# Attention on uncentred features in a graph kernel: vT = xT + hT times column-centred weights, scaled per node at evacuation, and the s2 row as a product of ones with a diagonal

## The chip, the cores and the metric

The kernel runs on one core of a Trainium2 chip. The metric is the device time of one execution, in microseconds; a profile is one more execution of the same program.

## The reference, cut to what matters

There are 64 graphs of 256 nodes with 256 features. Each passes three gated graph layers (GRU), a residual with layer norm, then graph attention, again with residual and layer norm.

```python
# layer 0: three times: m = h @ weight[i]; aggr = A.T @ m; h = GRU(aggr, h)
x = _layernorm(x + h, axis=-1)                 # called y below
# layer 1
Wh = jnp.matmul(x, W)
s1 = jnp.einsum('bnf,f->bn', Wh, a[:Fout, 0])
s2 = jnp.einsum('bnf,f->bn', Wh, a[Fout:, 0])
e = jax.nn.leaky_relu(s1[:, :, None] + s2[:, None, :], negative_slope=0.2)
attn = jax.nn.softmax(jnp.where(adj > 0, e, -9e15), axis=2)
x = _layernorm(x + jnp.matmul(attn, Wh), axis=-1)
```

## The kernel before

Graphs go through in pairs: 32 pairs, each of 512 nodes. A pair is a generator that yields between steps; two pairs are under way, half a pair apart, so that TensorE works on one pair's gates while other engines finish a step of the other pair. The scheduler that compiles the kernel may still reorder instructions; where I speak of the compiled order, I mean its result.

```python
    # pools for PSUM: four banks "t" for transposes, aggregation, attention; four "g" for gates
    def gates(i, e, ag, hT, hT_new, name):      # one half (128 features) of a layer's gates
        hn = product(2 * C + e, [hid])          # 2 + 4 + 2 + 4 = 12 f32 matmuls of 512 columns
        r_p = product(e, [hid, inp])
        n_p = product(2 * C + e, [inp])
        z_p = product(C + e, [hid, inp])
        # ACT: r, n, z; DVE: n, d*z, hT_new; POOL: d = hT - n
    ...
    def pair(p):
        hT = to_T(x_sb, f"xT_{p}")              # eight TensorE transposes
        yield
        for i in range(L):
            ag = aggregate(h, A, ...)           # eight f32 matmuls of 256 columns
            for e in range(C):
                gates(i, e, ag, hT, hT_new, ...)
                yield
            ...                                 # from_T(hT): eight transposes back to [node, feature]
            # last layer: v = h + x at evacuation on DVE, y = layer_norm(v)
            yield
        yT = to_T(y, f"yT_{p}")                 # eight transposes
        yield
        s2 = bank("s2")
        for d in range(C):                      # wa2: W @ a2 broadcast over 128 columns
            nc.tensor.matmul(s2, wa2[:, d, :], yT[:, d, :], start=(d == 0), stop=(d == C - 1))
        for k in range(K):                      # K = 4 blocks of 128 nodes
            pt = bank("pwh")
            for d in range(C):
                nc.tensor.matmul(pt[:, :D + 1], yT[:, d, k * P:(k + 1) * P], gw[:, d, :], ...)
            ...                                 # s1 and wh evacuated; scores = s2 + s1 on ACT
        ...                                     # leaky relu, mask, max on DVE, exp on ACT
        yield
        ...                                     # eT: eight transposes
        yield
        ...                                     # po = eT.T @ wh; residual; layer norm; store

    steps = 3 + 3 * L + 2                       # 14
    active, started = [], 0
    while started < NP or active:               # the next pair starts when the one has done 7 steps
        if started < NP and (not active or (len(active) == 1 and active[0][1] >= steps // 2)):
            active.append([pair(started), 0])
            started += 1
        for a in list(active):                  # one step of each
            ...
```

## Time and profile before

The median was 2843.95 us in three runs. What matters of the profile:

| per pair, TensorE | matmuls in the code | spacing |
|---|---|---|
| gates | 72, f32, 512 columns | 0.86 us each |
| aggregation | 24, f32, 256 columns | 0.43 us each |
| wh (with s1) | 8, f32, 257 columns | 0.43 us each |
| output product | 8, f32, 256 columns | 0.43 us each |
| s2 | 2, f32, 512 columns | 0.86 us each |
| transposes | 48 of 128 columns, 8 of them for y | 0.109 us each |

Spacing is the time from the start of one matmul's record to the next one's. An f32 matmul of the code is two records. The profile's mean durations are longer (592 ns for a record of 512 columns), because records overlap; for a TensorE that is the bound it is the spacing that adds up to the time. The spacings of all records sum, by construction, to the time from the first matmul to the last. A group's median spacing is its work, and what lies above it is waiting.

### The profile page before, as it was taken

To read this page: it belongs to the slowest core of one execution; us is meant where nothing else is said; L and a number is where in the kernel's file an instruction comes from. 1 tells how busy PE (TensorE), PEld (TensorE's weight loads), DVE (VectorE), ACT (ScalarE), POOL (GpSimd) and SP (SyncE) were. 2 spreads that over 40 slices of the span, in tenths; PEclk is the share of its full clock that TensorE was granted. 3 is DMA by queue.
4 is the path that set the end of the run, shared out by engine and by line. 5 is a ranking of instruction groups with operands and counts; after the bars stand their busy time and mean duration, and the time that the engine had idled before them with its cause. 6 is when DMAs were issued, how large, how long until landed. Compare 5 with 4: busy or idle time off the path is not lost.

```text
span 2842.6 us, 23364 instructions
## 1 busy us (share of the span) xinstructions
PE 2803.1 (99%) x8928; PEld 1560.3 (55%) x8928; DVE 1185.5 (42%) x2387; ACT 776.6 (27%) x1357; POOL 358.0 (13%) x362
## 2 busy tenths in 40 slices
PE   7999999999999999999999999999999999999996
PEld 4555555555555555555555555555555555555554
DVE  2344444444443444434443444443444444434434
ACT  1223222222322223222323222222222222222231
POOL 1111111111111111111111111111111111111111
PEclk9999999999999999999999999999999999999998
DMA  3000000000000000000000000000000000000000
GB/s 89 8 15 23 15 23 15 15 23 22 15 16 22 15 22 15 23 15 17 21 23 15 23 15 15 23 19 19 15 23 15 23 15 23 15 15 15 8 0 15
DMA packets 53518, 54.44 MB, mean 19 GB/s; under 512 B 1696, under 2 KB 53408, under 8 KB 53408
## 3 DMA queue, kind: packets, MB, share of 16 engines
q1 hardware_dynamic: 52256, 51.91, 5.6%
q8 instruction: 70, 1.15, 0.2%
q10 hardware_dynamic: 1056, 1.05, 0.1%
q14 instruction: 40, 0.33, 0.0%
q0 software_dynamic: 96, 0.01, 0.0%
HBM read 36.18 MB, written 16.78 MB: 19 GB/s over the span
## 4 chain that ended last, share of the span: by engine, by line
PE 98%; DVE 1%; DMA 0%; ACT 0%; issue 0%; POOL 0%; SPq 0%; POOLq 0%; DVEq 0%; ACTq 0%
PE pg L191 69%; PE pa L181 12%; PE pwh L270 4%; PE po L303 4%; PE pt L171 3%; PE s L263 2%; PE pt L162 2%; PE pt L294 1%; PE pw L138 1%; DMA adj<-in_adj_dram 0%; DVE d L210 0%; ACT z L207 0%; DVE hT L211 0%; PE pw L126 0%; DVE v L307 0%
## 5 line engine op out<-in xcount | busy, mean ns | idle before, releaser
L191 PE MATMUL pg<-ag,wc 128*128 128x512 f32 x2304 | 1051.4, 592 | 0.0
L191 PEld LDWEIGHTS pg<-ag,wc 128*128 128x128 f32 x2304 | 437.8, 190 | 551.0 <-issue 551.0
L191 PE MATMUL pg<-hT,whhT 128*128 128x512 f32 x1536 | 712.0, 592 | 0.0
L191 PEld LDWEIGHTS pg<-hT,whhT 128*128 128x128 f32 x1536 | 281.9, 190 | 278.8 <-issue 275.0
L202 DVE SCALAR_TENSOR_TENSOR n<-pg,bh,r 128x512 f32<-128x512 f32 x192 | 143.9, 750 | 603.8 <-ACT r L199 603.8
L199 ACT ACTIVATE r<-pg,b_sum 128x512 f32<-128x512 f32 x192 | 131.9, 687 | 859.8 <-PE pg L191 859.4
L191 PE MATMUL pg<-xT,whhT 128*128 128x512 f32 x768 | 350.5, 592 | 0.0
L210 DVE TENSOR_TENSOR d<-d,z 128x512 f32<-128x512 f32 x192 | 132.6, 691 | 522.0 <-ACT z L207 450.0
L209 POOL TENSOR_TENSOR d<-hT,n 128x512 f32<-128x512 f32 x128 | 162.1, 1267 | 1041.4 <-ACT n L204 1041.4
L181 PE MATMUL pa<-A,h 128*128 128x256 f32 x1024 | 239.3, 382 | 0.0
L204 ACT ACTIVATE n<-n,bi 128x512 f32<-128x512 f32 x192 | 138.5, 722 | 349.2 <-DVE n L203 349.2
L191 PEld LDWEIGHTS pg<-xT,whhT 128*128 128x128 f32 x768 | 143.5, 190 | 155.2 <-issue 146.1
L207 ACT ACTIVATE z<-pg,b_sum 128x512 f32<-128x512 f32 x192 | 132.1, 688 | 322.0 <-PE pg L191 322.0
L181 PEld LDWEIGHTS pa<-A,h 128*128 128x128 f32 x1024 | 191.9, 190 | 51.1 <-DVE h L72 12.1
L209 POOL TENSOR_TENSOR d<-xT,n 128x512 f32<-128x512 f32 x64 | 81.0, 1266 | 563.0 <-ACT n L204 563.0
L203 DVE TENSOR_TENSOR n<-n,pg 128x512 f32<-128x512 f32 x192 | 132.2, 689 | 32.5 <-PE pg L191 26.0
L211 DVE TENSOR_TENSOR hT<-d,n 128x512 f32<-128x512 f32 x192 | 131.9, 687 | 3.4
L171 PEld LDWEIGHTS pt<-ident,hT 128*128 128x128 f32 x768 | 88.4, 141 | 52.6 <-DVE hT L211 31.6
L270 PE MATMUL pwh<-gw,yT 128*128 128x257 f32 x512 | 116.7, 380 | 0.0
L303 PE MATMUL po<-wh,eT 128*128 128x256 f32 x512 | 116.5, 381 | 0.0
L181 PE MATMUL pa<-A,x 128*128 128x256 f32 x512 | 115.7, 379 | 0.0
L270 PEld LDWEIGHTS pwh<-gw,yT 128*128 128x128 f32 x512 | 97.5, 190 | 28.3 <-issue 8.5
(84 smaller groups left out, 1860.4 us busy)
## 6 DMA issues: line engine op xcount, KB each, us to landing
x<-in_x_dram SPq DMA_DIRECT2D x32, 512.0 KB, 3.8
adj<-in_adj_dram SPq DMA_DIRECT2D x32, 512.0 KB, 3.9
out_dram<-o SPq DMA_DIRECT2D x32, 512.0 KB, 2.9
wi_n<-in_L_gnn_w_ih_dram SPq DMA_DIRECT2D x1, 768.0 KB, 6.6
w_n<-in_L_gnn_weight_dram ACTq DMA_DIRECT2D x1, 768.0 KB, 9.4
wh_n<-in_L_gnn_w_hh_dram SPq DMA_DIRECT2D x1, 768.0 KB, 11.1
gw<-in_L_gnn_W_dram ACTq DMA_DIRECT2D x1, 256.0 KB, 10.4
bi<-in_L_gnn_b_ih_dram POOLq DMA_DIRECT2D x1, 3.0 KB, 8.1
```

The source lines that it names most:

```text
L171: nc.tensor.transpose(pt[:, (c * C + d) * P:(c * C + d + 1) * P], hT[:, d, (g * C + c) * P:(g * C + c + 1) * P], ident)
L181: nc.tensor.matmul(pt[:, g * N:(g + 1) * N], h[:, g, s, d * P:(d + 1) * P], A[:, g, s, :], start=(s == 0), stop=(s == C - 1))
L191: nc.tensor.matmul(pt, w[:, d, o * P:(o + 1) * P], m[:, d, :], start=(n == 0), stop=(n == len(todo) - 1))
L199: nc.scalar.activation(r, r_p, AF.Sigmoid, bias=b_sum[:, e:e + 1])
L202: nc.vector.scalar_tensor_tensor(n, hn, bh[:, 2 * C + e:2 * C + e + 1], r, op0=ALU.add, op1=ALU.mult)
L203: nc.vector.tensor_add(n, n, n_p)
L204: nc.scalar.activation(n, n, AF.Tanh, bias=bi[:, 2 * C + e:2 * C + e + 1])
L207: nc.scalar.activation(z, z_p, AF.Sigmoid, bias=b_sum[:, C + e:C + e + 1])
L209: nc.gpsimd.tensor_sub(d, hT[:, e, :], n)
L210: nc.vector.tensor_mul(d, d, z)
L270: nc.tensor.matmul(pt[:, :D + 1], yT[:, d, k * P:(k + 1) * P], gw[:, d, :], start=(d == 0), stop=(d == C - 1))
L303: nc.tensor.matmul(pt[:, c * D:(c + 1) * D], eT[:, g, j, c * P:(c + 1) * P], wh[:, g, j, :], start=(j == 0), stop=(j == C - 1))
```

## The change

The intent is to take work off TensorE. Layer norm is (v - mean) / std per node, so y @ W is v @ (W with its column means removed), times 1/std per node. So wh can be had from vT = xT + hT, which is there without transposing y, and the per-node scale is applied when ACT evacuates the product. s2 has then to be scaled per node too; it comes as one more column of wh and is turned into a row, the same on all partitions, as ones @ diag(s2), in two float32r products (the value rounded to float32r, and what remains).

The core of the diff (comments, the weights' preparation and names are cut):

```diff
-    gw = const.tile([P, C, D + 1], F32, name="gw")
-    wa2 = const.tile([P, C, P], F32, name="wa2")
+    gw = const.tile([P, C, D + 2], F32, name="gw")
+    gwc = const.tile([P, C, D + 2], F32, name="gwc")       # gw less its column means
+    ones = const.tile([P, P], F32R, name="ones")
 ...
-            else:
-                from_T(hT, ...)                            # v = h + x
-                y = work.tile(...)
-                layer_norm(v, y, f"a_{p}")
             yield
-        yT = to_T(y, f"yT_{p}")
-        yield
-        s2 = bank("s2")
-        for d in range(C):
-            nc.tensor.matmul(s2, wa2[:, d, :], yT[:, d, :], ...)
+        vT = work.tile([P, C, GN], F32, tag="hT", name=f"vT_{p}", bufs=4)
+        for d in range(C):
+            nc.gpsimd.tensor_add(vT[:, d, :], hT[:, d, :], xT[:, d, :])
+        from_T(vT, lambda g, pt: evacuate(v[:, g]...., pt))
+        rs = layer_norm(v, y, f"a_{p}")
+        yield
         for k in range(K):
             pt = bank("pwh")
             for d in range(C):
-                nc.tensor.matmul(pt[:, :D + 1], yT[...], gw[:, d, :], ...)
-            nc.vector.tensor_copy(s1[:, k:k + 1], pt[:, D:D + 1])
-            evacuate(wh[:, k // C, k % C, :], pt[:, :D])
-            nc.scalar.activation(sc[:, k, :], s2[...], AF.Identity, bias=s1[:, k:k + 1])
+                nc.tensor.matmul(pt[:, :D + 2], vT[...], gwc[:, d, :], ...)
+            nc.scalar.activation(wh[:, k, :], pt[:, :D + 2], AF.Identity, scale=rs[:, k:k + 1])
+        yield
+        s2 = work.tile([P, 2, K], F32R, ...)
+        nc.gpsimd.tensor_copy(s2[:, 0], wh[:, :, D + 1])
+        nc.gpsimd.tensor_sub(s2[:, 1], wh[:, :, D + 1], s2[:, 0])
+        dg = work.tile([P, 2, K, P], F32R, tag="dg", bufs=1)
+        for half in range(2):
+            nc.gpsimd.tensor_mul(dg[:, half], <ident, broadcast>, <s2[:, half], broadcast>)
+        s2b = bank("s2b")
+        for half in (1, 0):
+            nc.tensor.matmul(s2b, ones, dg[:, half]...., start=(half == 1), stop=(half == 0))
+        for k in range(K):
+            nc.scalar.activation(sc[:, k, :], s2b[...], AF.Identity, bias=wh[:, k, D:D + 1])
```

xT gets buffers of its own, and em has one buffer instead of two. A pair now has 15 steps, while `steps` still says 14: the offset between two pairs is 7 and 8 in turn.

More of the change, by code (lines that the diff above doesn't have):

```diff
@@ L9 @@
 F32 = mybir.dt.float32
+F32R = mybir.dt.float32r
 U8 = mybir.dt.uint8
@@ L91 @@
     wc = const.tile([P, L, C, O], F32, name="wc")
-    gw = const.tile([P, C, D + 1], F32, name="gw")
-    wa2 = const.tile([P, C, P], F32, name="wa2")
+    gw = const.tile([P, C, D + 2], F32, name="gw")
+    gwc = const.tile([P, C, D + 2], F32, name="gwc")
+    ones = const.tile([P, P], F32R, name="ones")
+    mean = const.tile([P, P], F32, name="mean")
+    nc.gpsimd.memset(mean, 1.0)
+    nc.gpsimd.tensor_copy(ones, mean)
+    nc.gpsimd.memset(mean, 1.0 / D)
     b_sum = const.tile([P, O // P], F32, name="b_sum")
@@ L147 @@
                                  start=(f == 0), stop=(f == C - 1))
-            wa = prep.tile([P, 2], F32, name=f"wa_{d}")
-            nc.vector.tensor_copy(wa, pt[:, :2])
-            nc.vector.tensor_copy(gw[:, d, D:D + 1], wa[:, 0:1])
-            nc.vector.tensor_copy(wa2[:, d, :], wa[:, 1:2].to_broadcast([P, P]))
+            nc.vector.tensor_copy(gw[:, d, D:], pt[:, :2])
+        pt = bank("pw")
+        for d in range(C):
+            nc.tensor.matmul(pt[:, :D + 2], mean, gw[:, d, :], start=(d == 0), stop=(d == C - 1))
+        for d in range(C):
+            nc.vector.tensor_sub(gwc[:, d, :], gw[:, d, :], pt[:, :D + 2])
     def to_T(src, name):
-        dst = work.tile([P, C, GN], F32, tag="hT", name=name, bufs=4)
+        dst = work.tile([P, C, GN], F32, tag="xT", name=name, bufs=2)
         for d in range(C):
@@ L226, in layer_norm @@
                                     mv[:, k, 0:1], rs[:, k:k + 1], op0=ALU.subtract, op1=ALU.mult)
+        return rs
     def pair(p):
@@ L236, in pair @@
             load(p + 1)
-        hT = to_T(x_sb, f"xT_{p}")
+        hT = xT = to_T(x_sb, f"xT_{p}")
         yield
@@ L250, in pair @@
                 from_T(hT, lambda g, pt: evacuate(h[:, g].rearrange("p c d -> p (c d)"), pt))
-            else:
-                from_T(hT, lambda g, pt: nc.vector.tensor_add(
-                    v[:, g].rearrange("p c d -> p (c d)"), pt, x_sb[:, g].rearrange("p c d -> p (c d)")))
-                y = work.tile([P, G, C, D], F32, tag="y", name=f"y_{p}")
-                layer_norm(v, y, f"a_{p}")
-            yield
-        yT = to_T(y, f"yT_{p}")
-        yield
-        s2 = bank("s2")
-        for d in range(C):
-            nc.tensor.matmul(s2, wa2[:, d, :], yT[:, d, :], start=(d == 0), stop=(d == C - 1))
-        wh = work.tile([P, G, C, D], F32, tag="wh", name=f"wh_{p}")
-        s1 = work.tile([P, K], F32, tag="s1", name=f"s1_{p}")
-        sc = work.tile([P, K, N], F32, tag="sc", name=f"sc_{p}")
+            yield
+        vT = work.tile([P, C, GN], F32, tag="hT", name=f"vT_{p}", bufs=4)
+        for d in range(C):
+            nc.gpsimd.tensor_add(vT[:, d, :], hT[:, d, :], xT[:, d, :])
+        from_T(vT, lambda g, pt: evacuate(v[:, g].rearrange("p c d -> p (c d)"), pt))
+        y = work.tile([P, G, C, D], F32, tag="y", name=f"y_{p}")
+        rs = layer_norm(v, y, f"a_{p}")
+        yield
+        wh = work.tile([P, K, D + 2], F32, tag="wh", name=f"wh_{p}")
         for k in range(K):
@@ L269, in pair @@
             for d in range(C):
-                nc.tensor.matmul(pt[:, :D + 1], yT[:, d, k * P:(k + 1) * P], gw[:, d, :],
+                nc.tensor.matmul(pt[:, :D + 2], vT[:, d, k * P:(k + 1) * P], gwc[:, d, :],
                                  start=(d == 0), stop=(d == C - 1))
-            nc.vector.tensor_copy(s1[:, k:k + 1], pt[:, D:D + 1])
-            evacuate(wh[:, k // C, k % C, :], pt[:, :D])
-            nc.scalar.activation(sc[:, k, :], s2[:, (k // C) * N:(k // C + 1) * N], AF.Identity,
-                                 bias=s1[:, k:k + 1])
+            nc.scalar.activation(wh[:, k, :], pt[:, :D + 2], AF.Identity, scale=rs[:, k:k + 1])
+        yield
+        s2 = work.tile([P, 2, K], F32R, tag="s2", name=f"s2_{p}")
+        nc.gpsimd.tensor_copy(s2[:, 0], wh[:, :, D + 1])
+        nc.gpsimd.tensor_sub(s2[:, 1], wh[:, :, D + 1], s2[:, 0])
+        dg = work.tile([P, 2, K, P], F32R, tag="dg", name=f"dg_{p}", bufs=1)
+        for half in range(2):
+            nc.gpsimd.tensor_mul(dg[:, half], ident.unsqueeze(1).to_broadcast([P, K, P]),
+                                 s2[:, half].unsqueeze(2).to_broadcast([P, K, P]))
+        s2b = bank("s2b")
+        for half in (1, 0):
+            nc.tensor.matmul(s2b, ones, dg[:, half].rearrange("p k j -> p (k j)"),
+                             start=(half == 1), stop=(half == 0))
+        sc = work.tile([P, K, N], F32, tag="sc", name=f"sc_{p}")
+        for k in range(K):
+            nc.scalar.activation(sc[:, k, :], s2b[:, (k // C) * N:(k // C + 1) * N], AF.Identity,
+                                 bias=wh[:, k, D:D + 1])
         nc.vector.scalar_tensor_tensor(sc, sc, ALPHA, sc, op0=ALU.mult, op1=ALU.max)
-        em = work.tile([P, K, N], F32, tag="em", name=f"em_{p}")
+        em = work.tile([P, K, N], F32, tag="em", name=f"em_{p}", bufs=1)
         nc.gpsimd.memset(em, NEG_INF)
@@ L302, in pair @@
                 for j in range(C):
-                    nc.tensor.matmul(pt[:, c * D:(c + 1) * D], eT[:, g, j, c * P:(c + 1) * P], wh[:, g, j, :],
+                    nc.tensor.matmul(pt[:, c * D:(c + 1) * D], eT[:, g, j, c * P:(c + 1) * P], wh[:, g * C + j, :D],
                                      start=(j == 0), stop=(j == C - 1))
```

## The prediction

> **What bounds the kernel now.** I read the page first, its line of busy time and its chain that ended last:
>
> ```profile
> PE 2803.1 (99%) x8928; PEld 1560.3 (55%) x8928; DVE 1185.5 (42%) x2387; ACT 776.6 (27%) x1357; POOL 358.0 (13%) x362
> ...
> PE 98%; DVE 1%; DMA 0%; ACT 0%; issue 0%; POOL 0%; SPq 0%; POOLq 0%; DVEq 0%; ACTq 0%
> ```
>
> TensorE is the bound: it is 98% of the chain, and the other engines have more than half their time free. A busy PE need not be one at its peak, so I then looked at the spacing of matmuls in the timeline, PE only, in the middle of the span (columns: start us, us, engine, line, operation, names, count):
>
> ```profile
> 1526.80 1.88 PE L191 MATMUL pg<-xT,whhT 128*128 128x512 f32 x4
> 1528.51 1.88 PE L191 MATMUL pg<-ag,wc 128*128 128x512 f32 x4
> 1530.23 1.04 PE L162 MATMUL pt<-ident,y 128*128 128x128 f32 x8
> 1531.10 0.38 PE L171 MATMUL pt<-ident,hT 128*128 128x128 f32 x2
> 1531.32 1.02 PE L191 MATMUL pg<-hT,whhT 128*128 128x512 f32 x2
> 1532.18 1.02 PE L263 MATMUL s<-yT,wa 128*128 128x512 f32 x2
> 1533.23 0.87 PE L171 MATMUL pt<-ident,hT 128*128 128x128 f32 x6
> 1533.94 1.02 PE L263 MATMUL s<-yT,wa 128*128 128x512 f32 x2
> 1534.80 3.64 PE L270 MATMUL pwh<-gw,yT 128*128 128x257 f32 x16
> 1538.27 1.89 PE L181 MATMUL pa<-A,h 128*128 128x256 f32 x8
> ```
>
> Each f32 matmul is two records, 0.43 us apart for 512 columns, so 0.86 us for one in the code; the eight transposes take 0.87 us; nothing is idle between rows but 0.1-0.2 us. In PE's waits the only long ones are in the first 20 us and after the last pair's gates (4.6 us for y, 6.6 us for the exponentials). So 31 of 32 pairs run with their attention hidden behind the other pair's gates, and PE time removed is gained one for one, if PE doesn't come to wait.
>
> **What the Trainium skill says.** "FP8 and Floating Point Precision", TensorE Precision Notes: true FP32 takes four passes through the array, and there is a reduced-precision one. "TensorE: Matmul & The Clock Gate", Back-to-back issue gap: 512 columns take 512/2.4 + 2.5 = 216 ns a pass when warm. Four passes are 0.86 us: the trace agrees. No page prices float32r; I estimate one pass, 0.22 us. "GPSIMD Engine Reference", Elementwise side-by-side: a two-input tensor_tensor costs about 2.6 cycles an element, and some 156 ns to start: 512 x 2.6 / 1.2 GHz + 156 = 1265 ns by estimate; the trace has 1267 ns, so I use that for the new 128x512 operations. The first page also says that matmuls keep program order (the queue pulls only weight loads ahead); so a matmul that waits holds all behind it.
>
> **The change, part by part** (per pair unless said; 32 pairs). The shapes and counts of what goes (columns: line, engine, operation, names, shapes, count, busy us, mean ns, idle before):
>
> ```profile
> L209 POOL TENSOR_TENSOR d<-hT,n 128x512 f32<-128x512 f32 x128 | 162.1, 1267 | 1041.4 <-ACT n L204 1041.4
> ...
> L263 PE MATMUL s<-yT,wa 128*128 128x512 f32 x128 | 67.2, 609 | 0.5 <-ACT yT L70 0.5
> ...
> L162 PE MATMUL pt<-ident,y 128*128 128x128 f32 x256 | 34.1, 277 | 4.6 <-DVE y L225 4.6
> ```
>
> - Gone from PE: y's transposes, 0.87 us, and two f32 matmuls for s2, 2 x 0.86 = 1.72 us. Sum 2.59 us.
> - New on PE: two float32r matmuls of 512 columns, 2 x 0.22 = 0.44 us. The eight transposes of the last h become eight of vT; pwh's 257 columns become 258: nothing.
> - Net 2.15 us a pair, 69 us in all. Had PE no new wait, 2844 - 69 = 2775 us, 2.4% less.
> - Elsewhere: POOL gains two adds, two products (1.27 us each) and two small operations (0.23 us as its smallest have); DVE loses copies; all of wh's evacuation goes to ACT. Not one of these is near a bound.
> - Prologue: two matmuls for the column means and a subtraction, +1.5 us. Tail: the last pair's chain loses y -> yT -> s2 and gains vT's add and the diagonal; by the tail's rows I get about 2 us less. They cancel.
>
> **Where the gain leaks.** What counts is the new order of waits. The changed pair has 15 steps against 14, and the next starts when one has done at least 7, so the offsets of pairs alternate between 7 and 8. The compiled order shows two patterns in turn, 16 pairs with offset 7, 15 with offset 8, and the last alone. I walk each with the trace's durations; t = 0 is where the second gate product z of the partner's layer 0 has been issued (1530.23 above).
>
> Offset 8. PE: eight pwh matmuls to t = 3.47, eight transposes of h to 4.34, one gate matmul to 5.20, then the float32r product, all others behind it. It needs: last pwh out of PE, 3.67; ACT's evacuation, 0.48 (a 128x256 one with a bias takes 478 ns), 4.15; POOL copy and subtraction, 0.23 each with 0.08 between, 4.77; two 128x512 products, the first one not waiting for the subtraction's end, 1.27 each, 7.33; 0.1 to PE: 7.4. **PE waits 2.2 us.** The products run from the low half first on PE, so both must be there. Before, s2 came straight from yT and had no such loop. 15 x 2.2 = 33 us.
>
> Offset 7. The float32r product comes only after the partner's next 12 gate matmuls, over 10 us later: no wait. But the layer norm is now in the way: vT's transposes 0 to 0.87, v's copies on DVE to 2.34, the partner's last h to 3.03, then statistics and power, 3.1 us in the tail's rows (2807.11 to 2810.22): the per-node scale is there at 6.1, the first evacuation at 6.65. PE has finished pwh at 6.26 and its next product, the aggregation, needs that bank (four banks in turn): 0.4 us. The transposes of h wait 0.2 us as before the change they did not; the exponentials come later (9.8 us after s2b, with 10.3 us of gates to hide them), which delays z by about 1.3 us and makes the output product wait 0.2 us at most. Together 0.9 us. 16 x 0.9 = 14 us.
>
> Sum: 2844 - 69 + 33 + 14 = 2822 us.
>
> **The rivals.** (1) PE stays without waits: 2775 us. For it: the reorder puts other matmuls ahead of most new waits, and before the change nothing waited. Against: the offset-8 order has only 1.7 us of PE work between pwh and the float32r product, and the chain there is 3.9 us. If POOL's products took half the time, 2800. (2) The float32r product costs as much as an f32 one (four passes): +1.3 us a pair, of which nothing is hidden: 2860 or so; no record of the kernel before can exclude it. (3) POOL holds up the gates: it is in order, and now a memset of the single em buffer (it must wait for the exponentials) stands ahead of a gate's subtraction. At offset 7 my walk has the partner's h at 34.05 and PE asking for it at 34.2: no slack. A microsecond too many in it costs 16 us: 2840. (4) Load on DVE or ACT: at 42% and 27% of time, and DVE loses work; I see nothing for it.
>
> **Range and chances.** I name 2820. The low end, 2785, is half of the waits gone and a bit more; the high end, 2848, has a further 1 us a pair. To be faster by over 2% the time must be under 2787, so the waits would have to be 12 us in all rather than 47: 0.13. Slower by over 2% means above 2901, waits of 126 us, 4 us a pair, or a float32r at full cost with these: 0.02. Within 2%: 0.85.
>
> **What would show it.** y's transposes and the s2 group gone; float32r records 64, about 0.22 us apart; PE busy about 70 us less; among PE's waits one of about 2.2 us, 15 times, s2b for POOL's diagonal; one of about 0.4 us, 16 times, for ACT's evacuation of wh; POOL's products at 1.27 us. Wrong if the s2b waits are absent (POOL or order quicker than I think), if the float32r records are wide, or if long waits stand at h's transposes or at the gates.

## The result, and the profile after

The changed kernel took 2798.07 us in the median of four runs (2796.78 to 2798.10), beside 2843.74 us of the kernel before in the same rounds. The ratio is 0.9838, 95% interval 0.9824 to 0.9852: 1.6% faster, which is within 2%.

The page of the changed kernel, busy time and chain that ended last:

```profile
PE 2733.8 (98%) x8612; PEld 1519.5 (54%) x8612; DVE 1143.7 (41%) x2129; ACT 799.9 (29%) x1421; POOL 512.6 (18%) x557
...
PE 93%; DVE 3%; POOL 2%; ACT 1%; DMA 0%; issue 0%; SPq 0%; POOLq 0%; DVEq 0%; ACTq 0%
```

PE is busy for 69 us less, and the time fell by only 46. The chain fell from 98% to 93% PE, with POOL, DVE and ACT taking up the difference: work of these now stands between TensorE and its next matmul. PE's waits (who waited, for whom, us in total, times, longest) name the largest:

```profile
PE s2b L291 <- POOL dg L287: 25.8, 16, 5.3
```

One of the 16 is the last pair's (5.3 us); the other 15 are 1.36 us each. The timeline of one of them, a pair at offset 8:

```profile
1422.04 3.65 PE L276 MATMUL pwh<-gwc,vT 128*128 128x258 f32 x16
...
1425.53 1.04 PE L179 MATMUL pt<-ident,hT 128*128 128x128 f32 x8
1425.73 0.48 ACT L278 ACTIVATE wh<-pwh,rs_a 128x258 f32<-128x258 f32 x1 [0.40 <-PE pwh L276]
...
1426.28 0.19 POOL L283 CAST s<-wh 128x4 fp32r<-128x4 f32 x1 [2.73 <-ACT wh L278]
1426.40 1.02 PE L199 MATMUL pg<-hT,whhT 128*128 128x512 f32 x2
1426.55 0.20 POOL L284 TENSOR_TENSOR s<-wh,s 128x4 fp32r<-128x4 f32 x1
...
1426.70 2.04 POOL L287 TENSOR_TENSOR dg<-ident,s 128x512 fp32r<-128x512 f32 x2
1428.79 0.73 PE L291 MATMUL s2b<-dg,ones 128*128 128x512 f32 x2 [1.36 <-POOL dg L287]
1429.37 3.62 PE L189 MATMUL pa<-A,h 128*128 128x256 f32 x16
```

After the last pwh matmul, PE has eight transposes and one gate matmul to do; these are issued by 1427.26. Meanwhile the last block of wh goes through ACT, then through four operations of POOL in a row, done at 1428.74. By the spacing PE loses 1428.79 - 1427.26 = 1.53 us; the profile says 1.36, since it counts the modelled end of the last matmul as busy.

At offset 7 the same product is far behind:

```profile
1510.71 2.78 PE L276 MATMUL pwh<-gwc,vT 128*128 128x258 f32 x12
...
1511.94 1.04 POOL L231 TENSOR_TENSOR rs_a<-rs_a,half 128x4 f32<-128x4 f32 x1
1513.01 1.58 ACT L278 ACTIVATE wh<-pwh,rs_a 128x258 f32<-128x258 f32 x4 [1.84 <-POOL rs_a L231]
...
1513.54 3.72 PE L189 MATMUL pa<-A,h 128*128 128x256 f32 x16
...
1524.82 1.88 PE L199 MATMUL pg<-ag,wc 128*128 128x512 f32 x4
...
1526.14 1.02 PE L291 MATMUL s2b<-dg,ones 128*128 128x512 f32 x2
...
1526.99 3.59 PE L199 MATMUL pg<-hT,whhT 128*128 128x512 f32 x8
```

Here the per-node scale is late instead: ACT's first evacuation waits for it until 1513.01, and the aggregation, which needs the freed bank, starts 0.21 us after PE could have had it. The s2b rows bear no wait. What the float32r product costs can be read here, where nothing waits. The four gate records from 1524.82 on are 4 x 0.43 us of work and would be done at 1526.54; the next gate record starts at 1526.99; so the two float32r records take 0.45 us, 0.23 us each. (Their row starts at 1526.14, because the profile sets the start of the first one 0.03 us after that of the gate record before it, in all such pairs; its spacing of 0.63 us to the second therefore takes in 0.40 us of that gate record.)

The whole account, from the sums of spacings (before to after, us): y's transposes -27.9 and s2's products -55.1, the float32r products 64 x 0.228 = +14.6, together **-68.4**; the s2b waits 15 x 1.53 = 22.9, with the start of the first product's weights 15 x 0.11 = 1.7, **+24.6**; at offset 7 16 x 0.38 (0.21 at the aggregation, 0.17 at h's transposes) **+6.2**; small gaps between the first gate matmul and the last, 16.2 before (6.1 at s2, 7.7 at the aggregation, 1.9 at h's transposes) and 7.2 after, **-9.0**; PE's waits in the last pair's tail, 19.7 before and 19.5 after, **-0.1**; a later start of the gates **+0.4**. The sum is -46.3, and so is the difference between the spans of the two profiles.

### The profile page after: what moved, and what is told of

Same layout as the page of the kernel before. It is cut to its first block, busy times and chain, and to the rows that moved or that the text cites. A ratio compares the mean times of both kernels' runs of the same rounds, so it can differ in the third digit from the quotient of the medians.

```text
span 2796.3 us, 22703 instructions
## 1 busy us (share of the span) xinstructions
PE 2733.8 (98%) x8612; PEld 1519.5 (54%) x8612; DVE 1143.7 (41%) x2129; ACT 799.9 (29%) x1421; POOL 512.6 (18%) x557
## 3 DMA queue, kind: packets, MB, share of 16 engines
q8 instruction: 68, 1.11, 0.2%
q10 hardware_dynamic: 1056, 1.05, 0.1%
## 4 chain that ended last, share of the span: by engine, by line
PE 93%; DVE 3%; POOL 2%; ACT 1%; DMA 0%; issue 0%; SPq 0%; POOLq 0%; DVEq 0%; ACTq 0%
PE pg L199 70%; PE pa L189 12%; PE po L324 4%; PE pwh L276 2%; PE pt L179 2%; POOL dg L287 1%; PE pt L315 1%; PE pt L170 1%; DVE st_a L227 1%; PE s2b L291 1%; PE pw L144 1%; POOL rs_a L231 1%; ACT wh L278 1%; ACT z L215 0%; DVE d L218 0%; DMA adj<-in_adj_dram 0%
## 5 line engine op out<-in xcount | busy, mean ns | idle before, releaser
L218 DVE TENSOR_TENSOR d<-d,z 128x512 f32<-128x512 f32 x192 | 159.9, 833 | 566.2 <-ACT z L215 519.0
L276 PE MATMUL pwh<-gwc,vT 128*128 128x258 f32 x512 | 119.6, 380 | 0.0
L324 PEld LDWEIGHTS po<-wh,eT 128*128 128x128 f32 x512 | 96.7, 192 | 26.5 <-issue 11.0
L73 DVE COPY ag<-pa 128x512 f32<-128x512 f32 x96 | 66.1, 688 | 109.2 <-PE pa L189 109.2
```

The costliest lines, as they stand in the source:

```text
L218: nc.vector.tensor_mul(d, d, z)
L276: nc.tensor.matmul(pt[:, :D + 2], vT[:, d, k * P:(k + 1) * P], gwc[:, d, :], start=(d == 0), stop=(d == C - 1))
L324: nc.tensor.matmul(pt[:, c * D:(c + 1) * D], eT[:, g, j, c * P:(c + 1) * P], wh[:, g * C + j, :D], start=(j == 0), stop=(j == C - 1))
```

## The experiments

My theory was that the missing part of the gain is the wait for the diagonal: at offset 8, chain of ACT and POOL less the TensorE work that the compiled order puts ahead of s2b. The rivals were a float32r product dearer than its spacing shows, the uneven offsets as such, and POOL's added load delaying the gates. Time of the kernel before was 2843.69 to 2844.07 us (medians) on the three chips used, so medians of runs may be compared. The 95% interval of a ratio is some 4 to 5 us wide to each side; where two runs differ by no more than that, it is the waits in their traces that tell them apart. Clear of 2% against the kernel before are apart, all7 and dg_dve (faster); one_f32 is unclear; all others are the same within 2%. All results were correct.

**Apart**: a step boundary more between wh and the diagonal, so that a whole gate step of the other pair lies between them.

```diff
             nc.scalar.activation(wh[:, k, :], pt[:, :D + 2], AF.Identity, scale=rs[:, k:k + 1])
         yield
+        yield
-    steps = 3 + 3 * L + 2
+    steps = 16
```

> One more step boundary between wh and the diagonal, 16 steps, so that every pair has a whole gate step of the other pair (over 10 us of TensorE) between the last pwh matmul and the float32r product, and the layer norm lies beside gates. Theory (what the change fails to gain is the wait of s2b for POOL's diagonal at offset 8, 15 x 1.5 to 1.7 us, and 0.4 us at offset 7 for the scale): both go, 2798 - 25 - 6 = 2767 us, between 2762 and 2775. Rival (the float32r product costs more than its spacing shows, or POOL's extra work delays the gates): the wait only turns up elsewhere, 2790 us or more.

Measured: 2760.53 us (2759.71 to 2761.72), ratio 0.9709 (0.9694 to 0.9723). It is 37.5 us faster than the change as it was, and beats both kernels. Its timeline where the wait had been:

```profile
1404.54 3.65 PE L276 MATMUL pwh<-gwc,vT 128*128 128x258 f32 x16
1408.03 1.04 PE L179 MATMUL pt<-ident,hT 128*128 128x128 f32 x8
1408.90 1.02 PE L199 MATMUL pg<-hT,whhT 128*128 128x512 f32 x2
1409.77 3.62 PE L189 MATMUL pa<-A,h 128*128 128x256 f32 x16
...
1422.26 1.02 PE L292 MATMUL s2b<-dg,ones 128*128 128x512 f32 x2
```

The starts follow one another at 16 x 0.217, 8 x 0.109 and 2 x 0.43 us: nothing is lost. The sums of spacings say the same for all 31 hidden pairs: no s2b wait, none at offset 7, and the small gaps at the aggregation (5.2 us) gone too, which is most of what it beat my expectation by. Only the last pair, with no partner, still waits.

**All8**: the empty step goes, so every pair has the pattern of offset 8.

```diff
                 from_T(hT, lambda g, pt: evacuate(h[:, g]...., pt))
-            yield
+                yield
```

> The empty step goes, 14 steps, so every pair has the order that has only one gate matmul between pwh and the float32r product. Theory: 31 waits of 1.5 to 1.7 us instead of 15, and no 0.4 us for the scale: 2798 + 16 x (1.6 - 0.4) = 2817 us, between 2812 and 2823. Rival (the alternation of offsets 7 and 8 costs in itself, by uneven pairs): no change or a gain, 2798 or less.

Measured: 2818.84 us, ratio 0.9913 (0.9899 to 0.9928). The wait row of its profile:

```profile
PE s2b L291 <- POOL dg L287: 45.7, 32, 3.6
```

By the spacings 31 waits of 1.52 us. Even offsets made the kernel slower, so it was not the unevenness that cost; the pattern did.

**All7**: all pairs in the pattern of offset 7 (an empty step ahead of vT, 16 steps).

```diff
+        yield
         vT = work.tile([P, C, GN], F32, tag="hT", name=f"vT_{p}", bufs=4)
-    steps = 3 + 3 * L + 2
+    steps = 16
```

> All pairs in the pattern of offset 7 (an empty step ahead of vT, 16 steps): the layer norm beside the light step, pwh before the per-node scale is there. Theory: no s2b waits, but the 0.38 us (0.21 at the aggregation, 0.17 at h's transposes) that the 16 pairs of the change show, 31 times: apart's 2760.5 + 12 = 2772 us, between 2769 and 2777. Rival (that pattern costs nothing): 2761 us.

Measured: 2776.76 us (2776.67 to 2778.58), at the upper end of what was expected. By the spacings 0.21 us at the aggregation and 0.17 us at h's transposes, 31 times, and 0.10 us more inside the aggregation, which I had not counted. So this pattern has its small price, and it's not the s2b product.

**Dg_dve**: the diagonal's two products on DVE.

```diff
-            nc.gpsimd.tensor_mul(dg[:, half], ...)
+            nc.vector.tensor_mul(dg[:, half], ...)
```

> The two products of the diagonal move from POOL to DVE. Theory (the length of the chain counts): two products at about 0.69 us instead of 1.04, and the compiled order puts two gate matmuls, not one, ahead of s2b at offset 8: the wait falls from 1.5 us to 0.1 to 0.8 us, 2776 to 2788 us. Rival (DVE is in order and its evacuations stand ahead): the wait stays at 1.4 us or more, 2796 us or more.

Measured: 2781.15 us, ratio 0.978 (0.9766 to 0.9795). Its timeline at a wait:

```profile
1080.57 0.69 DVE L287 TENSOR_TENSOR dg<-ident,s 128x512 fp32r<-128x512 f32 x1 [1.78 <-POOL s L283]
1080.62 0.70 POOL L284 TENSOR_TENSOR s<-wh,s 128x4 fp32r<-128x4 f32 x1
1081.18 0.68 DVE L73 COPY h<-pt 128x512 f32<-128x512 f32 x1
1081.79 0.68 DVE L287 TENSOR_TENSOR dg<-ident,s 128x512 fp32r<-128x512 f32 x1
1082.61 0.70 PE L291 MATMUL s2b<-dg,ones 128*128 128x512 f32 x2 [0.25 <-DVE dg L287]
```

The wait is 0.25 us instead of 1.36. Most of that isn't the engine: the compiled order has two gate matmuls ahead of s2b, 0.86 us more cover. The products take 0.69 us rather than 1.04, but POOL's small subtraction (0.70 instead of 0.20 us while a DVE product runs) and a copy of h come in between.

**Dg_more**: one product of the diagonal done twice.

```diff
-        for half in range(2):
+        for half in (0, 0, 1):
```

> One product of the diagonal is done twice on POOL (same result). Theory: each of the 15 waits at offset 8 grows by the 1.04 us of one product, the 16 pairs at offset 7 hide it: 2798 + 15 to 16 us = 2813 to 2815 us, s2b waits of about 2.4 us. Rival (the loss has another cause): under 3 us more.

Measured: 2803.37 us, only 5.3 us more than the change, where I expected 15 to 16. It did not test what I wanted, for the compiled order was no longer the same:

```profile
1089.10 0.50 PE L291 MATMUL s2b<-dg,ones 128*128 128x512 f32 x1 [1.37 <-POOL dg L287]
...
1090.10 0.50 PE L291 MATMUL s2b<-dg,ones 128*128 128x512 f32 x1
```

The first product waits as before (for two products of POOL) and an aggregation matmul now stands between the halves and hides most of the third. From the gate matmul ahead of s2b to the third aggregation record TensorE needs 0.33 us more than in the change (0.23 us of it the wait for the third product of POOL), 15 x 0.33 = 5.0 us; the tail takes 1.1 us more, and the gates start 0.7 us earlier.

**Chain_more**: the chain's first small copy five times in a row, which cannot be split.

```diff
-        nc.gpsimd.tensor_copy(s2[:, 0], wh[:, :, D + 1])
+        for _ in range(5):
+            nc.gpsimd.tensor_copy(s2[:, 0], wh[:, :, D + 1])
```

> The small copy that starts the diagonal's chain is done five times on POOL, same result: four more at 0.19 us and 0.08 us between, 1.1 us longer, with nothing that can slip between. Theory: each of the 15 waits at offset 8 grows by 1.1 us, the others hide it; with the last pair's tail 2798 + 16 x 1.1 = 2815 us, between 2811 and 2818. Rival (as dg_more seemed to say, a longer chain is mostly hidden): 2803 us or less.

Measured: 2801.74 us, 3.7 us more: the number I had given to the rival. The five copies took 1.19 us instead of 0.19, as intended, but the compiled order had answered again: two gate matmuls, not one, ahead of s2b. A chain 1.00 us longer less 0.86 us more cover is 0.14 us, and the wait in the timeline is 1.50 us against 1.36. So both misses left the rule standing only if cover is read from the compiled order each time, and that had to be tested with the order known beforehand.

**Chain_2 and chain_3**: the copy twice, which keeps the change's order, and three times, with which the second gate matmul moves ahead.

```diff
-        nc.gpsimd.tensor_copy(s2[:, 0], wh[:, :, D + 1])
+        for _ in range(2):        # chain_2;  range(3) in chain_3
+            nc.gpsimd.tensor_copy(s2[:, 0], wh[:, :, D + 1])
```

> The small copy twice instead of five times: the compiled order of TensorE is that of the change (one gate matmul between h's transposes and s2b; the five-fold one had got two there). Theory (wait at offset 8 = chain less TensorE work ahead of s2b): chain 0.25 us longer, same cover, 15 waits and the tail grow by 0.25 us: 2798 + 4 = 2802 us, s2b waits 1.6 us. Rival (POOL's chain doesn't set the wait): 2798 us.

> The small copy three times: a chain 0.5 us longer than in the change, but the compiled order puts a second gate matmul (0.86 us) ahead of s2b. Theory: the wait falls by 0.86 - 0.5 = 0.36 us to 1.0 us, so that more work on POOL makes the kernel faster: 2798 - 15 x 0.36 + 0.5 = 2793 us. Rival (a longer chain costs its length): 2803 us or more.

Measured: 2801.90 us (expected 2802) and 2793.36 us (expected 2793). A row of the timeline of each, chain_2 first:

```profile
1089.93 0.74 PE L292 MATMUL s2b<-dg,ones 128*128 128x512 f32 x2 [1.62 <-POOL dg L288]
```

```profile
1086.48 0.73 PE L292 MATMUL s2b<-dg,ones 128*128 128x512 f32 x2 [1.01 <-POOL dg L288]
```

The kernel with two useless copies more a pair is 4.7 us faster than the change, because its order changed. The theory's rule, wait = chain less cover, gave both signs and sizes. The times alone would be thin evidence (3.8 us slower and 4.7 us faster, beside intervals of 4 us), but between the first and the last gate matmul the sums of spacings changed by +3.8 and -5.3 us, and all of it is at the 15 waits (15 x 0.25 and 15 x -0.35 us).

**One_f32**: the diagonal in one f32 product; neither rounding nor remainder.

```diff
-        s2[:, 0] = copy, s2[:, 1] = remainder; two products into dg (float32r); two float32r matmuls
+        nc.gpsimd.tensor_mul(dg, <ident>, <wh[:, :, D + 1]>)       # f32, [P, K, P]
+        nc.tensor.matmul(s2b, ones, dg...., start=True, stop=True)  # ones in f32
```

> The diagonal in one f32 product instead of two float32r halves, schedule as in the change. The chain loses the copy, the subtraction and one product, 1.4 to 1.5 us, so that the wait at offset 8 all but goes (15 x 1.45 = 22 us, and 1.5 us in the tail); TensorE pays 0.86 instead of 0.45 us a pair, 13 us. Theory: 2798 - 23 + 13 = 2788 us, between 2783 and 2793. Rival (the float32r halves are what makes the gain, as the change says): over 2798 us. POOL's product at 1.04 us would say that the broadcast operands make it cheap, at 1.27 us that the float32r output does.

Measured: 2788.19 us, ratio 0.9804 (0.979 to 0.9819), the expected number. In the change's own schedule the single f32 product is 10 us better than the two halves, though TensorE works 13 us more, because the chain is shorter; once the wait is gone by the schedule (apart), the halves should be the better choice by these 13 us, which I didn't run. POOL's product in this run:

```profile
L283 POOL TENSOR_TENSOR dg<-ident,wh 128x512 f32<-128x512 f32 x32 | 33.5, 1047 | 74.0 <-ACT wh L278 74.0
```

With f32 output it takes 1.047 us, so the float32r output isn't what makes it quicker than the adds (1.26 us). Whether it is the broadcast operands or the multiplication stays open.

**Keep_y16 and keep_y**: only the s2 part of the change; y is normalized and transposed as before, wh comes from yT, 16 steps. The two differ in the place of the layer norm.

```diff
-        vT = ...; from_T(vT, ...); rs = layer_norm(...)
+        from_T(hT, <v = h + x>); layer_norm(v, y, ...)   # keep_y16: in the loop; keep_y: a step later
+        yT = to_T(y, ...); yield
-                nc.tensor.matmul(pt[:, :D + 2], vT[...], gwc[:, d, :], ...)
+                nc.tensor.matmul(pt[:, :D + 2], yT[...], gw[:, d, :], ...)
```

> Only the s2 part of the change, in the schedule of the run apart (16 steps, no wait before s2b): y is transposed as before, no vT, no per-node scale. Theory (TensorE time counts one for one once nothing waits): apart plus y's eight transposes of 0.109 us, 2760.5 + 32 x 0.87 = 2788 us, between 2785 and 2794. Rival (what the vT part saves lies on other engines or in waits): outside that.

> keep_y16 again (only the s2 part; y transposed), with the layer norm moved one step later beside a gate step, since in keep_y16 0.49 us a pair were lost at h's last transposes next to the following pair's start. Theory: apart's 2760.5 + 27.9 for y's transposes, plus gaps of 0.1 to 0.3 us a pair where y's and h's transposes meet: 2788 to 2798 us. Rival (the vT part saves more than TensorE time): over 2800 us.

Measured: 2808.48 us and 2800.11 us; both are above what I expected, 2788 and 2788 to 2798. Keep_y16 loses, by the spacings, 0.49 us a pair where h's last transposes meet the next pair's first aggregation (0.38 + 0.10 us, 31 times, 15 us). That place is gone in keep_y. What is left there over apart is 39.6 us: 27.9 us are y's transposes, some 7 us small gaps at h's transposes and pwh, and some 4 us the last pair's tail, in which y must be waited for. So against the better of these two schedules the vT part is worth about 40 us, not 28: the rivals were right that it saves more than the matmuls it removes (for keep_y only by 0.1 us over the 2800 us that I had set), and the rest, too, is TensorE's waiting around them. The steps of keep_y can't be those of apart, so part of this may be the schedule; a better place for y's transposes was not sought. The s2 part and the schedule together account for the other 44 us of apart's 83.

**Before16**: the kernel before with two empty steps, nothing else.

```diff
         yT = to_T(y, f"yT_{p}")
         yield
+        yield
 ...                                            # and one more after eT
-    steps = 3 + 3 * L + 2
+    steps = 16
```

> The kernel before with two empty steps (16 steps, offset 8), none of the change. It asks whether the kernel before could have had the part of apart's gain that comes of the schedule: its small gaps at s, at h's transposes and at the aggregation, 8.0, 4.3 and 7.9 us in the sums of spacings. If the gaps go with the schedule: about 2824 us. If they come of what the products need, 2838 to 2846 us.

Measured: 2859.83 us, ratio 1.0056 (1.0041 to 1.0071): 16 us slower, which neither of my two expectations had. The gaps at s2 and at the aggregation went, but others came (0.49 us a pair at h's last transposes as in keep_y16, 0.18 us at pwh, 0.15 us ahead of h's transposes). It shows that 16 steps alone are no gain, not that no schedule would help the kernel before; that stays open.

## Why the prediction was right, and where it was off

The forecast within 2% came true, and 2798 lies in the range of 2785 to 2848, but 22 us below the 2820 that I named. By its own steps:

- **TensorE work, net 2.15 us a pair, 69 us.** Right: 68.4 us by the spacings. The estimate of one pass for float32r was right too, 0.23 us a record against 0.22; rival (2) falls.
- **The wait at offset 8, 15 x 2.2 = 33 us.** The mechanism was right, in place, number and sign; the size was off. 15 waits of 1.53 us by the spacing, 22.9 us, and 1.7 us more in which the first product's weights are loaded. While s2b waits no other matmul starts (between 1426.84 and 1428.79 there is no PE record), so all others do stand behind it, as the walk says. The term that failed is "two 128x512 products ... 1.27 each": I took the duration of POOL's subtraction and the trace has 1.04, 0.46 us less for two; the small operations were 0.19 and 0.20 us rather than 0.23. Experiments apart, all8, chain_2 and chain_3 show that this wait is chain less cover, as the walk has it.
- **Offset 7, 16 x 0.9 = 14 us.** Too large: 0.38 us, 6 us. The aggregation lost 0.21 rather than 0.4, h's transposes 0.17 (0.2), the output product nothing (0.2 at most); these three parts add up to 0.8, not to the 0.9 of the walk. All7 shows that the loss belongs to the pattern.
- **Small gaps of the kernel before.** The reading "nothing is idle between rows but 0.1-0.2 us" took them for constant; they were up to 0.25 us a pair at s2, at h's transposes and at the aggregation, some 16 us in all, and 9 us of them went with the change. This step was missing. With the two above it, 8 us each, it makes the 24 us to the sum of 2822 (22 to the 2820 that I named); all three err to the same side, and none makes up for another.
- **Prologue and tail cancel.** Prologue: the first gate matmul starts 0.4 us later (47.45 to 47.83), not 1.5. Tail: from the last gate group's end to the end of the span 39.8 us before, 37.5 after, 2.3 less, about as worked out. But 2.1 us of it is TensorE work that the 69 us hold already; the waits stayed as they were, so there was little to cancel (+0.4 and -0.1 us).
- **Rival (3), POOL holding up the gates.** It didn't come, as far as PE's waits show; the slack held.

One cost was not foreseen, and is hidden: 31 of DVE's d*z products at 1.55 to 1.76 us rather than 0.69, each one overlapping POOL's adds for vT, as here:

```profile
1410.44 2.48 POOL L266 TENSOR_TENSOR vT<-hT,xT 128x512 f32<-128x512 f32 x2
...
1411.92 1.55 DVE L218 TENSOR_TENSOR d<-d,z 128x512 f32<-128x512 f32 x1 [3.60 <-ACT z L215]
```

The Trainium skill, "SBUF — State Buffer", Who interferes with whom, has it: the two engines share a port pair, which is an exclusive lock, and a DVE tensor_tensor with both inputs in SBUF contends with POOL's reads. The trace agrees: none of the 161 that did not meet POOL is long, all 31 that did are. In dg_dve one such product started 0.01 us ahead of an add, and there the add is the long one (1.80 instead of 1.26 us). No matmul waits for it here.

## What to carry to other kernels

When an engine that is the bound loses work, look at once at what the removed work had been covering: a chain through other engines costs its length less the bound engine's work that stands between its two ends in the compiled order. So read that order, not the source: here the scheduler answered a longer chain with more cover, and in chain_3 the longer chain was faster. And where two streams alternate, a step boundary in the right place can be worth nearly as much as the change itself: 37.5 us from one more boundary and the count of steps that fits it, beside 45.7 us from the change. The right place has to be found each time: two empty steps in the kernel before cost 16 us.

## What the Trainium skill lacked or had wrong

- No page gives the cost of a float32r matmul. Here two products of 512 columns with a 128x128 stationary operand take 0.45 to 0.47 us together, 0.23 us each, against 0.86 us for an f32 one (belongs to "TensorE: Matmul & The Clock Gate").
- "GPSIMD Engine Reference", Elementwise side-by-side, gives 2.6 cycles an element for two-input operations and no cost to start on this engine. At the 1.2 GHz of the page's own example that is an estimate of 1.11 us for 512 elements a partition; the adds and the subtraction took 1.26 to 1.27 us. A product of two broadcast operands took 1.04 to 1.05 us, with float32r and with f32 output alike; the page has no such case.
- "TensorE: Matmul & The Clock Gate", Part 4: PE-mode transpose, gives some 275 ns for a transpose (bf16) inside a kernel. The durations here agree (273 to 278 ns), but what adds up is the spacing, 0.109 us for f32, which the page does not give.
